# Cross attention: folding the queries of two heads over 64 rows each, into two banks

## The chip, the cores and the metric

The kernel runs on one core of a Trainium2 chip. The metric is the time of one execution on the device in microseconds (us), as the median over several runs. The engines of a core are named as in the profile: PE multiplies matrices (PEld are its weight loads), DVE does vector work, ACT activations and copies, POOL general work and gathers, SP issues transfers. PE writes its results into eight PSUM banks, each 128 partitions by 512 float32 numbers.

## What is computed

The reference is a stack of six parts on a residual stream `x` of 16 batches x 64 rows x 256 numbers: a sampled cross attention, a self attention and an expert layer, then a second cross attention, a recurrent layer and a second expert layer. The change lies in the second cross attention, with 16 heads of 64:

```python
q = (x @ Wq).reshape(B, N, HEADS, DIM_HEAD)
k = (ctx_txt @ Wk).reshape(B, TEXT_LEN, HEADS, DIM_HEAD)
v = (ctx_txt @ Wv).reshape(B, TEXT_LEN, HEADS, DIM_HEAD)
out = _attend(q, k, v)
Li = ctx_img.shape[1]
k_ip = (ctx_img @ Wk_ip).reshape(B, Li, HEADS, DIM_HEAD)
v_ip = (ctx_img @ Wv_ip).reshape(B, Li, HEADS, DIM_HEAD)
out_ip = _attend(q, k_ip, v_ip)
out = out + IMG_SCALE * out_ip
return out @ Wo + bo
```

`ctx_txt` are the first 77 rows of a batch's context, `ctx_img` the other 1524. `_attend` is a softmax attention with the scale 1/8.

## The kernel before, in words

For the 1524 image rows the kernel does not form the keys. It folds the key weights of a head into that head's queries instead: q k^T = (q Wk_ip^T) ctx^T, so the folded queries, 256 numbers for each of 64 queries, are multiplied with the turned context directly. The values are treated in the same way: the probabilities are multiplied with the context itself, and the value weights come after.

The class `Cross` does this in steps. A step is one pair of heads of one batch: 16 batches x 8 pairs = 128 steps, in the order of the counter `n`. In a step the 128 columns are 2 heads x 64 queries. Engines PE, DVE and ACT run in the order in which the code is written; nothing reorders it. A step `n` (line 1124 on) issues, for PE:

- 24 matmuls that give the scores of pair `n` (line 88, `st<-qf,cT`): 12 chunks of 128 context rows, two halves of 256, into three banks of their own pool of four. After each bank DVE takes a maximum (line 1144). Between the second and the third bank stands the turning of the result of pair `n - 2`.
- `out(n - 2)` (line 1074): value weights for two heads, each into 64 partitions of one bank.
- the product of probabilities and context of pair `n - 1`, in three parts of four chunks each (line 1113), into one bank that stays open over all three parts. Between the first and second part stands the transpose of the maximum (line 1163), and between the second and third part its transpose back (line 1173) and `fold(n + 2)`.

After line 1173 ACT copies the maximum (`mc`, line 1175), then `fold`'s result (line 1072); DVE subtracts `mc` from the scores (line 1184) and ACT takes the exponential (line 1185) of each of three banks in turn. These are the probabilities `pt` that the next step's product reads. `step` takes up to four generators of other stages' work (`side`, `mid`, `more`, `late`), which put their own instructions in between; the one called `late` stands between the exponentials and the third part of the product.

The fold of a pair works on `qbd`, a tile that holds for each pair and batch a block diagonal: partitions 0 to 63 have the first head's 64 queries in columns 0 to 63 and zeros in the others, partitions 64 to 127 the second head's in columns 64 to 127. The zeros are written once, when the tiles are made; `queries` (line 1009) fills only the blocks. With the zeros, one matmul over all 128 partitions (64 rows of the key weights of one head and 64 of the other) gives both heads' folded queries side by side, 128 columns. There are two such matmuls a fold, one for each half of the 256 context numbers, and their result is copied in one piece. The same tile `qbd`, zeros and all, is what `text` (line 1031) takes as its stationary side for the 77 text rows.

The weights come as `wk`, four pairs in one tile, loaded from memory by SP two times a batch. Two folds are issued ahead of the first step, in `ahead` (line 1221). All matmul results but the scores share a pool of four banks, taken with `bank()`; a bank is free again once what reads it is done.

Of the kernel before, what the change touches and what calls it, by code (L numbers as in the profile page):

```python
# [17 lines left out]
P = 128  # L18
B, S, D = 16, 64, 256
M = 1601  # L20
KC = D // P
# [13 lines left out]
H1, HD1, INNER, TEXT = 16, 64, 1024, 77  # L35
# [30 lines left out]
def perceiver_kernel(ctx: ExitStack, tc: tile.TileContext, a: dict, out: bass.AP):  # L66
    nc = tc.nc

    def mk(pool, shape, tag, dtype=F32, bufs=None):
        return pool.tile(list(shape), dtype, tag=tag, name=tag, bufs=bufs)  # L70
# [71 lines left out]
    def bank():  # L142
        return mk(pmm, [P, 512], "mm")
# [73 lines left out]
    qbds = []  # L217
# [51 lines left out]
    for j in range(2):  # L269
        r = slice(j * S, (j + 1) * S)  # L270
# [688 lines left out]
    class Cross:  # L959
# [100 lines left out]
        def fold(self, n):  # L1060

            if n >= B * NHP:
                return
            b, hp = divmod(n, NHP)
            w = self.w[b, hp // 4]
            rhs = qbds[b // 2 % 2][:, hp, b % 2].rearrange("p h q -> p (h q)")
            pf = bank()
            for k in range(KC):
                nc.tensor.matmul(pf[:, k * P : (k + 1) * P], lhsT=w[:, hp % 4, k * P : (k + 1) * P], rhs=rhs,  # L1069
                                 start=True, stop=True)  # L1070
            qf = self.qf[n] = mk(self.xc, [P, KC, P], "qf", bufs=3)
            nc.scalar.copy(qf.rearrange("p c n -> p (c n)"), pf[:, : KC * P])  # L1072

        def out(self, n):

# [788 lines left out]
```

## Time and profile before

| what | value |
|---|---|
| time, median of 3 runs | 2980.36 us (2976.62 to 2980.77) |
| profiled execution | 2978.07 us, of which 2976.4 us are its span |
| PE busy | 2811.3 us, 94% of the span |
| PEld busy | 2344.9 us, 79% |
| DVE busy | 1626.4 us, 55% |
| ACT busy | 1071.7 us, 36% |
| POOL busy | 830.4 us, 28% |
| share of the chain of waits that lies on PE | 76% |
| granted clock of PE, mean | 0.98 |
| fold's matmuls, line 1069 | records of 275 ns in the median, 762.6 to 2655.0 us, and 8 records before that |
| fold's copy, line 1072 | 128 copies of 128x256, 373 ns each |

A profile of this kind lists, for one execution, every instruction with its engine, its line in the kernel, the tiles it writes and reads, and its duration. Sizes such as `128*128 128x257` at a matmul mean 128 rows and 128 columns of the stationary side, and a moving side of 128 rows by 257 columns. Every float32 matmul has two records, each with a weight load. Matmuls overlap, and their ends are modelled: a record's duration is longer than the time by which it puts off the next, so distances between starts say more than durations. The chain of waits follows the execution back from its last instruction; what stands in it sets the end. The windows table gives each engine's busy time in stretches of the execution, and the timeline merges equal instructions that follow each other into one row with their number.

### The profile page before, as it was taken

Reading aid. Unit: us, or ns where it says so; the run is one execution under the profiler, and the core shown is the slowest. Engines: PE = TensorE matmul, PEld = TensorE weight load, DVE = VectorE, ACT = ScalarE, POOL = GpSimd, SP = SyncE. Lnnn points to the kernel's source line nnn. Section 1 sums busy time; section 2 is a strip of 40 time slices with the busy share of each in tenths; the row PEclk is TensorE's granted clock in tenths of the full one; section 3 lists DMA queues with packets and bytes.
Section 4 is the critical chain, followed back from the end, with each engine's and each line's share of the span. In section 5 each row is a group of like instructions: output and inputs, shape, how many; then the busy total and the mean of one; then the engine's idle time right before and its main releaser. Section 6 shows DMA issues by size and latency. Waiting matters only on the chain.

```text
span 2976.4 us, 46295 instructions
## 1 busy us (share of the span) xinstructions
PE 2811.3 (94%) x17734; PEld 2344.9 (79%) x17734; DVE 1626.4 (55%) x4138; ACT 1071.7 (36%) x2427; POOL 830.4 (28%) x923
## 2 busy tenths in 40 slices
PE   8999999796899988999999999999999999997799
PEld 4554466464788877899999999999999999994687
DVE  3344443533566655332557754686544785655856
ACT  3443433542223443333343332443232443222431
POOL 0677777777771000000101100020000010001723
PEclk9999999998899999999999999999999999999999
DMA  7666766476322101465212111121111221005753
GB/s 218 180 193 201 225 184 195 137 236 183 77 69 63 49 10 41 135 192 167 70 50 80 52 33 52 55 71 55 38 33 47 66 64 51 8 1 161 218 151 110
DMA packets 324853, 313.97 MB, mean 105 GB/s; under 512 B 57989, under 2 KB 275881, under 8 KB 324121
## 3 DMA queue, kind: packets, MB, share of 16 engines
q1 hardware_dynamic: 172137, 213.05, 22.5%
q10 hardware_dynamic: 126928, 63.06, 7.5%
q0 software_dynamic: 25568, 34.91, 5.3%
q8 instruction: 141, 2.31, 0.3%
q14 instruction: 79, 0.65, 0.1%
HBM read 236.31 MB, written 74.62 MB: 104 GB/s over the span
## 4 chain that ended last, share of the span: by engine, by line
PE 76%; DVE 8%; POOL 6%; issue 3%; DMA 3%; ACT 3%; SPq 1%; ACTq 0%; DVEq 0%; POOLq 0%
PE st L88 31%; PE mm L1113 21%; PE mm L88 14%; POOL g L446 6%; PE mm L153 4%; PE mm L1069 2%; DMA g<-tab,ig 2%; DVE hs L1359 1%; PE mm L1099 1%; DVE hc L1364 1%; PE mm L1038 1%; ACT pt L1185 1%; DVE db L1357 1%; DVE mp L1144 1%; PE mm L1163 1%
## 5 line engine op out<-in xcount | busy, mean ns | idle before, releaser
L1113 PE MATMUL mm<-cn,pt 128*128 128x257 f32 (+1 forms) x3072 | 741.6, 385 | 1.2 <-ACT cT L82 1.2
L88 PE MATMUL st<-qf,cT 128*128 128x128 f32 x6144 | 739.9, 278 | 0.0
L88 PEld LDWEIGHTS st<-qf,cT 128*128 128x128 f32 x6144 | 721.3, 194 | 3.3 <-ACT qf L1072 0.2
L446 POOL DMA_INDIRECT g<-tab,ig x640 | 620.2, 969 | 282.1 <-issue 176.9
L1113 PEld LDWEIGHTS mm<-cn,pt 128*128 128x128 f32 (+1 forms) x3072 | 555.4, 190 | 84.6 <-ACT cT L82 2.3
L88 PE MATMUL st<-wkv,cxt 128*128 128x512 f32 (+1 forms) x832 | 377.1, 598 | 1.0 <-ACT cxt L415 1.0
L1144 DVE TENSOR_REDUCE mp<-st 128x128 f32<-128x512 f32 x384 | 260.4, 688 | 214.5 <-PE st L88 214.1
L1184 DVE TENSOR_TENSOR pt<-st,mc 128x512 f32<-128x512 f32 (+1 forms) x384 | 224.2, 639 | 152.2 <-ACT mc L1175 152.2
L88 PEld LDWEIGHTS st<-wkv,cxt 128*128 128x128 f32 (+1 forms) x832 | 149.1, 187 | 157.6 <-issue 155.9
L1185 ACT ACTIVATE pt<-pt 128x512 f32<-128x512 f32 (+1 forms) x384 | 207.5, 588 | 51.9 <-DVE pt L1184 51.6
L399 ACT COPY kv<-st 128x512 f32<-128x512 f32 (+1 forms) x208 | 121.3, 588 | 190.2 <-PE st L88 189.6
L1175 ACT COPY mc<-mm 128x128 f32<-128x128 f32 x128 | 34.2, 267 | 385.3 <-PE mm L1173 384.8
L972 POOL MEMSET cn<- 128x12 f32 x16 | 2.0, 122 | 590.6 <-PE mm L1113 584.1
L1122 ACT COPY ot<-mm 128x256 f32<-128x256 f32 x128 | 47.5, 371 | 311.2 <-PE mm L153 311.1
L1165 DVE TENSOR_REDUCE xmx<-mm 128x1 f32<-128x128 f32 x128 | 37.4, 292 | 193.4 <-PE mm L1163 193.4
L1465 POOL DMA_INDIRECT xb<-xnd,row x55 | 59.6, 1084 | 281.8 <-PE mm L1099 217.8
L1365 POOL TENSOR_TENSOR mn<-mn,hc 128x512 f32<-128x512 f32 x64 | 84.1, 1314 | 173.4 <-DVE hc L1364 165.2
L1089 ACT COPY yt<-mm 128x64 f32<-128x64 f32 x128 | 27.2, 213 | 248.4 <-PE mm L88 248.4
L88 PEld LDWEIGHTS mm<-xt,w 128*128 128x128 f32 x512 | 83.0, 197 | 26.0 <-issue 14.4
L88 PE MATMUL mm<-xt,w 128*128 128x256 f32 (+1 forms) x512 | 94.8, 333 | 3.3 <-DVE act L886 3.3
L1347 POOL MEMSET da<- 128x8 f32 x64 | 7.5, 117 | 319.3 <-ACT da L1346 319.0
L1359 DVE TENSOR_TENSOR_SCAN hs<-da,db 128x512 f32<-128x512 f32 x64 | 79.3, 1239 | 7.0 <-DVE db L1357 0.5
(469 smaller groups left out, 3978.1 us busy)
## 6 DMA issues: line engine op xcount, KB each, us to landing
tab<-kv ACTq DMA_DIRECT2D x48, 1024.0 KB
w<-in_gate SPq DMA_DIRECT2D x66, 512.0 KB
cx<-in_ctx SPq DMA_DIRECT2D x48, 512.0 KB
cn<-in_ctx SPq DMA_DIRECT2D x16, 1408.0 KB
w<-in_lin SPq DMA_DIRECT2D x33, 512.0 KB
wk<-in_xwkiT SPq DMA_DIRECT2D x32, 512.0 KB
wg<-in_guT SPq DMA_DIRECT2D x55, 256.0 KB
g<-tab,ig POOLq DMA_INDIRECT x640
```

What stands on the lines that cost most here:

```text
L88: nc.tensor.matmul(o, lhsT=l, rhs=r, start=i == 0, stop=i == len(pairs) - 1)
L153: nc.tensor.transpose(t[:ncol, i, :rows], b, ident[:rows, :rows])
L399: nc.scalar.copy(kv[:w, :, c, :], pk[:w].rearrange("p (h e) -> p h e", h=H0))
L446: nc.gpsimd.indirect_dma_start(out=gf[:, (half * n + s) * 4 * HD0 : (half * n + s + 1) * 4 * HD0], out_offset=None, in_=tables[j], in_offs ...
L1069: nc.tensor.matmul(pf[:, k * P : (k + 1) * P], lhsT=w[:, hp % 4, k * P : (k + 1) * P], rhs=rhs, start=True, stop=True)
L1113: nc.tensor.matmul(po, lhsT=pt[:w, c, :], rhs=cn[:w, c, :], start=c == 0, stop=c == NCH - 1)
L1144: nc.vector.tensor_reduce(mp_[:, i, :], s.rearrange("p c n -> p n c"), AX.X, ALU.max)
L1184: nc.vector.tensor_tensor(o, st[i][:, :m, :], mc.to_broadcast([P, m, P]), ALU.subtract)
L1185: nc.scalar.activation(o, o, AF.Exp)
L1359: nc.vector.tensor_tensor_scan(hs.rearrange("p c n -> p (c n)"), da.rearrange("p c n -> p (c n)"), db.rearrange("p c n -> p (c n)"), 0.0, ...
L1365: nc.gpsimd.tensor_tensor(y, y, hc, ALU.add)
L1465: nc.gpsimd.indirect_dma_start(out=x, out_offset=None, in_=xnd, in_offset=bass.IndirectOffsetOnAxis(ap=tb.row[:, i : i + 1], axis=0))
```

## The change

The fold no longer multiplies over all 128 partitions with the zeros in. Each head gets matmuls of its own, over its own 64 partitions of the weights and of `qbd`, with 64 moving columns in place of 128. The two heads take turns, and each writes into a bank of its own, so a fold takes two of the four banks. Its result is copied in two pieces, one for each head, into the same tile `qf` as before.

```diff
-            rhs = qbds[b // 2 % 2][:, hp, b % 2].rearrange("p h q -> p (h q)")
-            pf = bank()
+            pf = [bank(), bank()]
+
             for k in range(KC):
-                nc.tensor.matmul(pf[:, k * P : (k + 1) * P], lhsT=w[:, hp % 4, k * P : (k + 1) * P], rhs=rhs,
-                                 start=True, stop=True)
+                for h in range(2):
+                    r = slice(h * HD1, (h + 1) * HD1)
+                    nc.tensor.matmul(pf[h][:, k * S : (k + 1) * S], lhsT=w[r, hp % 4, k * P : (k + 1) * P],
+                                     rhs=qbds[b // 2 % 2][r, hp, b % 2, h, :], start=True, stop=True)
             qf = self.qf[n] = mk(self.xc, [P, KC, P], "qf", bufs=3)
-            nc.scalar.copy(qf.rearrange("p c n -> p (c n)"), pf[:, : KC * P])
+            for h in range(2):
+                nc.scalar.copy(qf[:, :, h * S : (h + 1) * S], pf[h][:, : KC * S].rearrange("p (k q) -> p k q", q=S))
```

Here `KC` is 2, `P` 128, `S` 64 (queries of a batch) and `HD1` 64 (size of a head). The tile `qbd`, its zeros and `text`, which reads them, are left as they were.

## The prediction

> **What bounds the kernel now.** I read the busy table first, then the windows table over the stretch in which the changed function runs, then the chain of waits, and last the timeline of one step. The changed function, `fold`, has the line 1069 (its matmuls) and 1072 (its copy); it runs from 753 to 2655 us.
>
> ```profile
> core 0: us, PE busy (x) PEld busy (x) DVE busy (x) ACT busy (x) POOL busy (x), PEclk, DMA share, GB/s
> 762.00:955.00 193.00, 183.18 (x1371) 168.43 (x1369) 129.78 (x332) 57.30 (x143) 108.89 (x118) 0.98 0.24 61
> 955.00:1160.00 205.00, 182.20 (x1202) 163.35 (x1203) 118.25 (x372) 91.39 (x196) 0.12 (x1) 0.93 0.11 34
> 1160.00:2676.00 1516.00, 1507.06 (x11252) 1387.84 (x11251) 880.50 (x2020) 523.33 (x1247) 94.76 (x144) 1.00 0.22 66
> ```
>
> The reader is to see that from 1160 us on PE is idle for 9 of 1516 us, at a granted clock of 1.00; DVE and ACT have 42% and 65% to spare. The chain of waits in one step of this stretch is PE alone:
>
> ```profile
> 1508.23 0.11 PE mm L1173
> 1508.34 0.45 PE mm L1069 x4
> 1508.78 1.74 PE mm L1113 x8
> ```
>
> So what is added to PE's stream between line 1173 and line 1113 is added to the end, step by step. Now PE and its weight loads (PEld) around that fold:
>
> ```profile
> 1508.07 0.27 PE L1173 MATMUL mm<-ident,xmx 128*128 128x128 f32 x1
> 1508.07 0.52 PEld L1069 LDWEIGHTS mm<-qbd,wk 128*128 128x128 f32 x4
> 1508.17 0.61 PE L1069 MATMUL mm<-qbd,wk 128*128 128x128 f32 x4
> ...
> 1508.51 0.96 PEld L1113 LDWEIGHTS mm<-cn,pt 128*128 128x128 f32 x5
> 1508.62 1.03 PE L1113 MATMUL mm<-cn,pt 128*128 128x257 f32 x4
> ```
>
> Each f32 matmul leaves two records, each with a load of its own: two matmuls, x4. One load lasts 0.192 us, so four loads in 0.52 start (0.52 - 0.19) / 3 = 0.11 us apart. The first load starts together with the matmul before it (1508.07 both), and line 1113's first load together with fold's last matmul (1508.17 + 0.61 - 0.275 = 1508.505). Loads are hidden behind the matmuls ahead of them. From the transpose of line 1173 to the product's first matmul it is 1508.62 - 1508.07 = 0.55 us; in nearly all of the 126 steps that fold it is the same within 0.01.
>
> **What the narrower moving side is worth.** After the change each matmul moves 64 columns in place of 128, but its stationary side keeps 128 columns. What such a record costs is seen where the moving side is narrow already, in a router product with 8 columns:
>
> ```profile
> 568.17 0.52 PEld L88 LDWEIGHTS mm<-rws,xt 128*128 128x128 f32 x4 [1.28 <-ACT xt L173]
> 568.18 0.61 PE L88 MATMUL mm<-rws,xt 128*128 128x8 f32 x4 [1.05 <-ACT xt L173]
> ```
>
> Four loads in 0.52 again: 0.11 us apart, with 8 moving columns as with 128. The load sets the pace. So halving the moving side saves nothing by itself, and the change makes 8 records of 4. Run one after another they take 8 x 0.11 = 0.89 us in place of 0.44.
>
> **Two halves side by side.** The eight are two independent sets of four: rows 0 to 63 for one head, rows 64 to 127 for the other, each into its own bank. Before has no matmul on a row half, but it has one on column halves in the same order (two records on the first, two on the second):
>
> ```profile
> 18.11 0.19 PEld L291 LDWEIGHTS mm<-dg,ones 16*64 16x64 f32 x4 [0.76 <-issue]
> ```
>
> A load of 64 columns lasts 0.13 and back to back they start 0.055 apart (two of line 88's in 0.19), so one after another four would take 0.13 + 3 x 0.055 = 0.30. They took 0.19: two and two at a time. I take the row halves as running side by side too: 4 x 0.11 = 0.44 us, what fold takes now. The bound above is 0.89, the bound below 4 x 0.055 = 0.22, if half the rows loaded in half the time, as half the columns do.
>
> **The change of shape.** The step already leaves the full array once, for `out`, whose results go to 64 partitions:
>
> ```profile
> 1502.10 0.50 PE L88 MATMUL st<-qf,cT 128*128 128x128 f32 x3
> ...
> 1502.81 0.45 PE L88 MATMUL mm<-ot,wvi 128*64 128x64 f32 x6
> ...
> 1502.53 0.19 PEld L88 LDWEIGHTS mm<-ptt,vt 77*64 77x64 f32 x2
> ...
> 1502.70 0.19 PEld L88 LDWEIGHTS mm<-ptt,vt 77*64 77x64 f32 x2
> ...
> 1503.19 0.51 PEld L1113 LDWEIGHTS mm<-cn,pt 128*128 128x128 f32 x3
> ```
>
> Going in: the last full matmul starts at 1502.10 + 0.50 - 0.275 = 1502.325, and the next load not with it but at 1502.53, 0.205 later. Coming out: the last half-wide matmul starts at 1502.81 + 0.45 - 0.22 = 1503.04, the next load at 1503.19, 0.15 later. Neither load is hidden: the array first runs empty. Over all steps of the trace these two gaps hold within 0.01 us, also where the load waits for no semaphore, so it is the shape and not a wait.
>
> Fold gets both. After: 0.205 until the first load, 0.11 for that load, 3 x 0.11 to the last matmul's start, 0.15 until the product's load, 0.11 for it: 0.905 us. Less 0.555: +0.35 us a fold. Between the two heads' tiles the shape stays, so I count nothing there (the column halves above show none).
>
> The Trainium skill bears on this at one place. No row of before has a row half; its page "TensorEngine Tiling (Array Packing)", section "Key Properties", says that a change of tiling mode drains the engine and a change of tile within a mode doesn't. By it the sum stands, +0.35. The same page's table of theoretical speedups gives up to twice the rate where the contraction is 64 or less; by that alone fold would go from 0.44 to an estimated 0.22 us. The load rows here, 0.11 us with 8 moving columns, are why I don't take it.
>
> **The sum.** 128 folds (as many copies of line 1072): 126 inside steps, two ahead of the first, which share one change of shape. 126 x 0.35 + 0.4 = 44.5 us. Eleven of them lie between 955 and 1160 us, where PE has 23 us of idle time, much of it for side chains of other engines; I let a third of their delay vanish there: -1.3. Sum +43 us.
>
> **What is hidden.** One copy of 256 columns (line 1072, 373 ns) becomes two of 128. The nearest row is line 1175, 267 ns: 2 x 267 - 373 = +161 ns a fold on ACT, 20 us in all. Behind them on ACT stand the exponentials of line 1185, which wait for DVE's first subtraction (from 1508.67, 0.69 us) anyway; PE needs their result at the next step's product, over 5 us later, and qf two steps later. Cover: ACT's idle 65%. Without that cover it would be +20 us. The second bank: of the four that matmuls share, the product's and the maximum's are taken at fold, so the two heads take the others, which ACT's copy in `out` and DVE's reduction have left microseconds earlier. Who comes next into these banks waits for ACT's second copy, some 0.75 us after fold; PE has 1.74 us of product to run first. In some 17 steps side work stands in between, its first bank is the maximum's, free by then; bound 17 x 0.75 = 13 us, taken as 0. The zeros are still written once, and `text` still reads them: nothing is saved there. No DMA moves.
>
> The profiled execution had 2976.4 us of span, 2978.07 in all, 2.3 under the median of 2980.36. On the median: **2980.4 + 43 = 3023 us**. Offsets between the halves of 0.11 (one record) or 0.17 (what `out`'s second half shows, 1502.70 against 1502.53) give +0.46 or +0.52 a fold, 3038 or 3046.
>
> **Rivals.**
> - The halves do not overlap: 8 x 0.11. Then +0.35 + 0.445 = +0.79 us a fold, +100 us, 3080. Against it: the column halves above. For it: a load of 128 columns sets the pace, and two may share one path; no row shows two of that width at once.
> - No draining for row halves: 0.44 against 0.44, no change, 2980. Against it: every smaller shape in the trace shows such gaps, those of 16, 17 and 23 rows (lines 291 and 653) among them: 0.10 to 0.13 us from their last matmul to the next load.
> - The other side: half the rows load in half the time, and the array isn't drained. 0.22 us less a fold, 128 x 0.22 = 28 us less: 2952. It decides from a fold of under 0.50 us between line 1173 and the product, 6 us in all. For it: the 64-column loads at half the pace; against it: both its parts must hold.
> - ACT as the bound: +20 us on top, 3043; against it its idle share.
>
> **Chances.** Side by side with draining, 3016 to 3030: 0.66. With an offset or with ACT's copies in the open, to 3046: 0.13. One after another: 0.10. No change: 0.04. Faster: 0.05. The rest, between 2990 and 3012: 0.02. About 0.2% (6 us) is what a measurement here can tell from no change. Range 3012 to 3046 holds the first two, 0.79. Slower: 0.66 + 0.13 + 0.10 + 0.02 = 0.91.
>
> **What would show it.** In the timeline, fold's first load starts 0.20 us after line 1173's transpose and not with it; its matmuls come in pairs a few ns apart, pairs 0.11 apart; the product's first load comes 0.15 after the last. Line 1113's share of the chain stays, PE's busy time grows by some 43 us or less (modelled ends hide the empty array), two copies of about 267 ns stand per fold. Wrong if the pairs are 0.055 apart, if eight starts are evenly 0.11 apart, or if the loads start with the matmul before them.

## The result: slower by 39 us, and the profile after

The changed kernel takes 3018.25 us (median of 4 runs, 3011.67 to 3020.12); before took 2979.03 us (median of 4, 2976.62 to 2980.77). The ratio is 1.0128, with a 95% interval of 1.011 to 1.0146. The profiled execution has a span of 3018.4 us, 42.0 more than that of before.

The windows table of the changed kernel, over the late part of the stretch with folds (columns: the window, its length, busy time and instructions of each engine, granted clock, share and rate of transfers):

```profile
core 0: us, PE busy (x) PEld busy (x) DVE busy (x) ACT busy (x) POOL busy (x), PEclk, DMA share, GB/s
1160.00:2718.00 1558.00, 1549.63 (x11682) 1402.67 (x11682) 889.11 (x2037) 530.14 (x1350) 94.73 (x144) 1.00 0.21 65
```

PE is still idle for only 8 us, at a granted clock of 1.00; DVE's busy time rises by 9 and ACT's by 7 us. The stretch is 42 us longer, and PE fills it. At its start the changed kernel is already 7 us behind (the 25th transpose of its line 1176 starts at 1165.0 us, before's 25th of line 1173 at 1158.5). From the first of these transposes to the last it takes 43.6 us more than before; the first one starts 2.2 us earlier. The timeline of one step of the changed kernel, around the fold (its line is now 1071, the transpose's 1176, the product's 1116):

```profile
1801.62 0.27 PE L1176 MATMUL mm<-ident,xmx 128*128 128x128 f32 x1
...
1801.82 0.52 PEld L1071 LDWEIGHTS mm<-qbd,wk 64*128 64x128 f32 x8 [0.28 <-issue]
1801.82 0.66 PE L1071 MATMUL mm<-qbd,wk 64*128 64x64 f32 x8
1801.98 0.27 ACT L1178 COPY mc<-mm 128x128 f32<-128x128 f32 x1 [3.74 <-PE mm L1176]
...
1802.41 0.95 PEld L1116 LDWEIGHTS mm<-cn,pt 128*128 128x128 f32 x5
1802.41 1.14 PE L1116 MATMUL mm<-cn,pt 128*128 128x257 f32 x4
1802.51 0.43 ACT L1075 COPY qf<-mm 128x128 f32<-128x128 f32 x2 [0.26 <-PE mm L1071]
```

Three things are to be seen. Eight loads take 0.52 us, as four did before: they run two and two, (0.52 - 0.19) / 3 = 0.11 us from pair to pair; in the single records the two loads of a pair start 6 to 7 ns apart. The first load starts 0.20 us after the transpose, where before it started with it. And the product's first load comes 1802.41 - 1801.62 = 0.79 us after the transpose, where before it came 0.44 after; now it isn't hidden either, for the product's first matmul record starts with it. In the single records, which the timeline merges, the product's second matmul starts 1.11 us after the transpose, 0.77 before: +0.34 us a fold, and 126 x 0.34 = 43 us. The chain of waits has the same place:

```profile
1801.78 0.11 PE mm L1176
1801.89 0.59 PE mm L1071 x8
1802.48 1.94 PE mm L1116 x8
```

Before it stood there as 0.11, 0.45 and 1.74: the fold's piece is 0.14 longer and the product's, which now holds a load that nothing hides, 0.20.

### The profile page after: what moved, and what is told of

Same layout as the page of the kernel before. It is cut to its first block, busy times and chain, and to the rows that moved or that the text cites. A ratio compares the mean times of both kernels' runs of the same rounds, so it can differ in the third digit from the quotient of the medians.

```text
span 3018.4 us, 47507 instructions
## 1 busy us (share of the span) xinstructions
PE 2857.2 (95%) x18246; PEld 2355.1 (78%) x18246; DVE 1633.7 (54%) x4138; ACT 1080.3 (36%) x2555; POOL 827.5 (27%) x923
## 4 chain that ended last, share of the span: by engine, by line
PE 82%; DVE 6%; POOL 3%; DMA 3%; ACT 3%; issue 2%; SPq 1%; ACTq 0%; DVEq 0%; POOLq 0%
PE st L88 34%; PE mm L1116 23%; PE mm L88 15%; PE mm L153 5%; POOL g L446 3%; PE mm L1071 3%; DMA g<-tab,ig 1%; PE mm L1102 1%; PE mm L1038 1%; DVE hs L1362 1%; DVE hc L1367 1%; PE mm L1166 1%; ACT pt L1188 1%; PE mm L1176 0%; DVE db L1360 0%
## 5 line engine op out<-in xcount | busy, mean ns | idle before, releaser
L1116 PE MATMUL mm<-cn,pt 128*128 128x257 f32 (+1 forms) x3072 | 756.2, 390 | 1.0 <-ACT cT L82 1.0
L1071 PEld LDWEIGHTS mm<-qbd,wk 64*128 64x128 f32 x1008 | 68.1, 187 | 36.1 <-issue 31.0
```

The source lines that it names most:

```text
L1071: nc.tensor.matmul(pf[h][:, k * S : (k + 1) * S], lhsT=w[r, hp % 4, k * P : (k + 1) * P], rhs=qbds[b // 2 % 2][r, hp, b % 2, h, :], start= ...
L1116: nc.tensor.matmul(po, lhsT=pt[:w, c, :], rhs=cn[:w, c, :], start=c == 0, stop=c == NCH - 1)
```

## The experiments

All experiments ran on three other chips than the first comparison. On these the same kernel before took 3265 to 3299 us: the part up to the first fold is some 225 to 255 us longer there and scatters. So each whole time is compared with before on its own chip, and beside it I give a stretch in which PE is hardly ever idle (busy for 1195.7 of 1200.1 us in before): the 87 steps from the 41st transpose of line 1173 to the last (starts of records in the trace; for before 1478.79 and 2678.86 us). Before took 1200.1 us for it on the first chip and again 1200.1 on a later one, after 1228.1 on both. It holds 86 folds; in e6 the fold's new place leaves 85.

| kernel | whole, us | before on the same chip, us | ratio (95% interval) | 87 steps, us | against before |
|---|---|---|---|---|---|
| after, first chip | 3018.25 | 2979.03 | 1.0128 (1.011 to 1.0146) | 1228.1 | +28.0 |
| a0_after_again | 3309.58 | 3266.67 | 1.0139 (1.0105 to 1.0173) | 1228.1 | +28.0 |
| e1_full_rows | 3358.04 | 3299.13 | 1.0176 (1.0138 to 1.0213) | 1236.7 | +36.6 |
| e2_one_half | 3381.7 | 3299.13 | 1.0241 (1.0211 to 1.0272) | 1264.1 | +64.0 |
| e3_two_a_visit | 3325.81 | 3299.13 | 1.0069 (1.0032 to 1.0106) | 1214.9 | +14.8 |
| e4_two_copies | 3297.84 | 3299.13 | 1.0005 (0.9977 to 1.0034) | 1200.1 | 0.0 |
| e5_head_by_head | 3312.9 | 3265.41 | 1.0148 (1.0107 to 1.0189) | 1228.6 | +28.5 |
| e6_after_out | 3305.04 | 3265.41 | 1.011 (1.0071 to 1.0148) | 1210.7 | +10.6 |
| e7_two_batches | 3281.79 | 3265.41 | 1.0047 (1.0023 to 1.007) | 1197.1 | -3.0 |
| e8_two_batches_after_out | 3277.27 | 3265.41 | 1.0029 (1.0007 to 1.0052) | 1188.5 | -11.6 |
| e9_two_batches_full | 3278.09 | 3266.67 | 1.0039 (1.0008 to 1.007) | 1197.9 | -2.2 |
| e10_late_start | 3267.95 | 3266.67 | 1.001 (0.9992 to 1.0028) | 1188.5 | -11.6 |

In e7 to e10 the 87 steps hold less work: 40 visits, which are 80 folds and not 86, since six pairs of heads of the stretch were folded ahead of it. At 0.44 us a fold of before that alone is 6 x 0.44 = 2.7 us. For these kernels a second stretch counts: from the turning of a result (`mm<-ident,os`) in step 46 to that in step 126, 80 steps with 80 folds in every kernel.

| kernel | 80 steps with equal work, us | against before |
|---|---|---|
| before (both chips) | 1104.9 | |
| after (both chips) | 1130.9 | +26.0 |
| e6_after_out | 1115.3 | +10.4 |
| e7_two_batches | 1104.6 | -0.3 |
| e8_two_batches_after_out, e10_late_start | 1096.1 | -8.8 |
| e9_two_batches_full | 1105.4 | +0.5 |

**The load's pace alone.** Four narrow matmuls a fold, but over all rows, so that the shape never changes:

```diff
-                    r = slice(h * HD1, (h + 1) * HD1)
-                    nc.tensor.matmul(pf[h][:, k * S : (k + 1) * S], lhsT=w[r, hp % 4, k * P : (k + 1) * P],
-                                     rhs=qbds[b // 2 % 2][r, hp, b % 2, h, :], start=True, stop=True)
+                    nc.tensor.matmul(pf[h][:, k * S : (k + 1) * S], lhsT=w[:, hp % 4, k * P : (k + 1) * P],
+                                     rhs=qbds[b // 2 % 2][:, hp, b % 2, h, :], start=True, stop=True)
```

> Four matmuls a fold with 64 moving columns each, into two banks, but over all 128 rows, zeros included: no change of shape. Theory (a load of 128 columns sets a pace of 0.11 us, a smaller shape empties the array): eight loads one after another, 0.89 us in place of 0.44, no empty array: +0.445 x 126 = +56 on before, 3035. Rival (half the moving columns take half the time): as before, 2979.

Timeline of this kernel (its fold is line 1070, the transpose 1175, the product 1115):

```profile
2366.54 0.27 PE L1175 MATMUL mm<-ident,xmx 128*128 128x128 f32 x1
2367.49 1.52 PE L1115 MATMUL mm<-cn,pt 128*128 128x257 f32 x6
...
2366.54 0.97 PEld L1070 LDWEIGHTS mm<-qbd,wk 128*128 128x128 f32 x8
```

Eight loads in 0.97: (0.97 - 0.19) / 7 = 0.11 apart, though each matmul moves half as many columns. The first starts with the transpose: no gap. From the transpose to the product's matmul it is 0.95, +0.40 on before; 36.6 / 86 = 0.43 a fold in the 87 steps, and +59 in the whole where 56 were expected. The rival falls: narrower moving sides are worth nothing under a load of 128 columns. Twice the records without the two halves are dearer than the change.

**The overlap taken away.** Both heads' matmuls on rows 0 to 63 (with another pair's weights for the second, so that no load repeats); the second head's queries are left out:

```diff
+            r = slice(0, HD1)
             for k in range(KC):
                 for h in range(2):
-                    r = slice(h * HD1, (h + 1) * HD1)
-                    nc.tensor.matmul(pf[h][:, k * S : (k + 1) * S], lhsT=w[r, hp % 4, k * P : (k + 1) * P],
-                                     rhs=qbds[b // 2 % 2][r, hp, b % 2, h, :], start=True, stop=True)
+                    nc.tensor.matmul(pf[h][:, k * S : (k + 1) * S], lhsT=w[r, (hp + h) % 4, k * P : (k + 1) * P],
+                                     rhs=qbds[b // 2 % 2][r, hp, b % 2, 0, :], start=True, stop=True)
```

> All four matmuls of a fold on rows 0 to 63, so the second head's queries are not folded: nothing can run side by side. Theory: the empty array of after stays (0.34 us a fold), and eight loads follow one another, 0.44 us more: 126 x 0.785 = +99 on before, 3078. Rival (64 rows load in half the time, and nothing runs side by side in after either): as after, 3018.

Timeline of this kernel:

```profile
2369.99 0.27 PE L1176 MATMUL mm<-ident,xmx 128*128 128x128 f32 x1
...
2370.19 0.96 PEld L1071 LDWEIGHTS mm<-qbd,wk 64*128 64x128 f32 x8 [0.28 <-issue]
2371.22 0.95 PEld L1116 LDWEIGHTS mm<-cn,pt 128*128 128x128 f32 x5
```

The same two gaps (0.20 going in), and between them eight loads one after another: 0.96 where the change has 0.52. The 87 steps grow by 64.0 / 86 = 0.74 us a fold, 0.79 expected; the whole by 83, less than the 99 expected, with an interval that leaves 70 to 90. Rows of 64 load no faster than rows of 128: the rival falls. What after gains by running side by side is thus 1264.1 - 1228.1 = 36 us in these steps.

**The emptying halved.** Two folds together in every second step; `pf` is viewed as two folds by two halves of the context numbers:

```diff
-            self.fold(n + 2)
+            if n % 2:
+                self.fold([n + 1, n + 2])
```

> As after, but two folds together in every second step, into the same two banks. Theory: the array is emptied half as often, 63 x 0.34 = +21 on before, 3000. Rival (the loss lies in the number of records or copies): unchanged, 3018.

Timeline of this kernel (fold 1072, transpose 1178, product 1118):

```profile
2369.36 0.27 PE L1178 MATMUL mm<-ident,xmx 128*128 128x128 f32 x1
2369.56 1.11 PE L1072 MATMUL mm<-qbd,wk 64*128 64x64 f32 x16
...
2370.60 0.95 PEld L1118 LDWEIGHTS mm<-cn,pt 128*128 128x128 f32 x5
```

Sixteen records, twice those of the change, and the product's load comes 1.24 us after the transpose: 0.45 more than the change's 0.79 and not twice it. The 87 steps lose 14.8 instead of 28.0, close to the half. The cost goes by visits, not by records, matmuls or copies. The whole lost 27, with an interval from 11 to 35; 21 were expected.

**The copies alone.** Before's two matmuls and one bank, with the copy in two pieces:

```diff
-            nc.scalar.copy(qf.rearrange("p c n -> p (c n)"), pf[:, : KC * P])
+            for h in range(2):
+                nc.scalar.copy(qf[:, :, h * S : (h + 1) * S],
+                               pf[:, : KC * P].rearrange("p (k h q) -> p k h q", k=KC, h=2)[:, :, h, :])
```

> Before, with ACT's copy alone made in two pieces. Theory: hidden, 2979, within 3. Rival (ACT's longer queue holds up the exponentials): up to +20, 2999.

1.0005, and the 87 steps agree with before to the tenth. ACT's 20 us are hidden; nothing of the loss is theirs.

**The order of the heads.** The two loops changed round:

```diff
-            for k in range(KC):
-                for h in range(2):
+            for h in range(2):
+                for k in range(KC):
```

> As after, but both matmuls of the first head stand ahead of both of the second: four records on one half, then four on the other. Theory: PE looks ahead past a busy half, as in the step's out; the second half starts at most 0.17 us late: 3018 to 3040. Rival (records start in the order of the program): the halves follow one another, +0.44 x 126 on after for the most part, 3055 to 3074.

Timeline of this kernel:

```profile
2332.30 0.67 PE L1071 MATMUL mm<-qbd,wk 64*128 64x64 f32 x8
...
2332.30 0.53 PEld L1071 LDWEIGHTS mm<-qbd,wk 64*128 64x128 f32 x8 [0.28 <-issue]
```

Eight loads in 0.53 again, though four for the first half stand ahead of four for the second; on one half alone eight took 0.96 (e2). "In turns" isn't needed: records of the second half start beside those of the first, not behind them. So the order of the code does not fix the order of the starts. The names in before's `out` show the same: the second head's loads `ptt` start at 1502.70 us, though six more records of `ot` follow, two of them the first head's. 1228.6 against 1228.1 in the 87 steps.

**The fold moved behind `out`**, which has left the full array already:

```diff
                 self.out(n - 2)
+            self.fold(n + 2)
...
-            self.fold(n + 2)
```

> As after, but the fold stands right behind out, whose matmuls already left the full array: the array is emptied three times a step in place of four. Theory: from out's last matmul the fold adds its own loads and one emptying, 0.59 us, in place of 0.44 in before: +0.15 x 126 = +19 on before, 2998. Rival (going from column halves to row halves costs as much as through the full array): 3018.

Timeline of this kernel, from `out` to the product:

```profile
2006.49 0.45 PE L88 MATMUL mm<-ot,wvi 128*64 128x64 f32 x6
...
2006.87 0.52 PEld L1071 LDWEIGHTS mm<-qbd,wk 64*128 64x128 f32 x8
2007.46 1.17 PEld L1116 LDWEIGHTS mm<-cn,pt 128*128 128x128 f32 x6
```

From column halves to row halves the gap is there too (last matmul 2006.49 + 0.45 - 0.22 = 2006.72, next load 2006.87: 0.15), so it is paid at this change of shape too. But the way back from `out` was paid before, so the fold adds only 2007.46 - 2006.87 = 0.59. In the 87 steps it loses 10.6 us, 0.12 a fold, 0.15 expected; after lost 28.0. The whole lost 40 and not 19, as much as the rival would: its first 12 steps (from the first transpose to the 13th) took 227 us. With the fold at its old place in every step they took 199 to 215 (b0, a0, e5, e4, e1, e2), but also 223 in e3, where it stands in every second. That is what the last runs looked into.

**Two batches in a visit.** Batches 2t and 2t + 1 use the same weights and lie side by side in `qbd`. Folding both at once gives 128 moving columns, so that the load's pace is no longer wasted:

```diff
+                    nc.tensor.matmul(pf[h][:, k * q : (k + 1) * q].rearrange("p (b q) -> p b q", q=S),
+                                     lhsT=w[r, hp % 4, k * P : (k + 1) * P],
+                                     rhs=qbds[b // 2 % 2][r, hp, bs[0] : bs[-1] + 1, h, :], start=True, stop=True)
...
+                if bb:
+                    qf = mk(self.xp, [P, KC, P], "qo", bufs=8)
```

> Row halves with 128 moving columns: the two batches of a pair share the weights, so one visit in the even batch's steps folds both, and the odd batch's steps fold nothing; 62 visits instead of 126. The folded queries of the odd batch wait in 8 tiles, paid for with single buffers for the weights and the text values. Theory: a visit costs 0.79 us where two folds of before cost 0.89: -0.1 x 62 = -6 on before, 2973. Rival (two halves cannot move 128 columns each side by side): +0.44 a visit, 3001.

> As the run with two batches in a visit, but the visit stands right behind out. Theory: 0.59 us a visit where two folds of before cost 0.89: -0.3 x 62 = -18 on before, 2960, faster than both kernels. Rival (no gain from the shared emptying): 2973.

> Two batches in a visit as in e7, with the same buffers and loads, but over all 128 rows with the zeros, 256 moving columns: no change of shape. Control for what the grouping alone does. Theory: four records at the pace of 256 columns, 0.217 us, 0.87 us a visit where two folds of before cost 0.89: the 87 steps from the 41st transpose of line 1173 to the last as in before, 1200 us, within 2, and the whole as before. Rival (e7 and e8 gain by the halved weight loads or the fewer visits and not by the row halves): as e7, 1197, or less.

Timelines of e7 and of e9, both with the visit at the old place:

```profile
2316.35 0.27 PE L1191 MATMUL mm<-ident,xmx 128*128 128x128 f32 x1
2316.55 0.71 PE L1079 MATMUL mm<-qbd,wk 64*128 64x128 f32 x8
...
2317.19 1.39 PEld L1131 LDWEIGHTS mm<-cn,pt 128*128 128x128 f32 x7
```

```profile
2331.09 0.27 PE L1188 MATMUL mm<-ident,xmx 128*128 128x128 f32 x1
2331.20 1.03 PE L1077 MATMUL mm<-qbd,wk 128*128 128x256 f32 x4
...
2331.85 1.49 PEld L1128 LDWEIGHTS mm<-cn,pt 128*128 128x128 f32 x7
```

The row halves move 128 columns each side by side: two folds in place of the change's one, 0.05 us later at the product's load (0.84 after the transpose, 0.79 in the change). The rival of e7 falls. At the old place neither form gains: on equal work e7 is 0.3 us below before and e9, the same grouping with the zeros, 0.5 above, so the emptying takes what the row halves save. The 3.0 and 2.2 us of the 87 steps are little more than the six folds made ahead; by these steps alone e9 stands between its theory (1200, within 2) and its rival (1197), on equal work it stands with its theory.

Behind `out`, in e8:

```profile
2072.19 0.45 PE L88 MATMUL mm<-ot,wvi 128*64 128x64 f32 x6
2072.57 0.71 PE L1079 MATMUL mm<-qbd,wk 64*128 64x128 f32 x8
2073.22 1.14 PE L1131 MATMUL mm<-cn,pt 128*128 128x257 f32 x4
```

A visit takes 2073.22 - 2072.57 = 0.65 us, not the 0.59 of e6's 64 columns, against 0.89 for two folds of before. On equal work e8 saves 8.8 us, 0.22 for each of 40 visits, 0.30 expected. So in the stretch that PE bounds, e8 is faster than both kernels. The whole times missed their expectations: e7, e8 and e9 are 0.3 to 0.5% slower than before on their chips.

**Where e8 gave it back.** e10 is e8 with the visit at its old place in the first 12 steps:

```diff
+            if n >= 12:
+                self.fold(n + 2)
...
+            if n < 12:
+                self.fold(n + 2)
```

> Two batches in a visit right behind out, as e8, but in the first 12 steps, where gathers and loads run beside, the visit keeps its old place. Theory: the 87 steps as e8, 1188.5 us, 11.6 below before; the first 12 steps no longer than before's; the whole 15 to 18 below before on the same chip. Rival (the loss of e8's first steps is not the place of the fold): the first 12 steps some 10 us longer than before's again, the whole within 5 of before.

> The changed kernel, unaltered, on the same chip as the two above. Theory: the 87 steps take 1228 us, 28 more than before, whatever the chip; the whole +39 to +43 on before. Rival (on a chip with slower transfers the early stage takes part of it up): less than +30 in the whole.

> Before, unaltered, for its profile on the same chip: the first 12 steps and the 87 late steps to set beside the others. Both theories: 87 steps in 1200 us; the time up to the first fold as in the three above, within 15.

Before again (b0) and after again (a0) repeat the 87 steps to the tenth, and after's +43 on before in the whole is what the first chip showed. From the 13th transpose to the end e10's profile takes 2047.5 us, b0's 2064.7: 17 less, what was expected of the whole. Its first 12 steps took 208 us, e8's 225, b0's 199, a0's 208; e7 and e9, with the visit at the old place throughout, 207 and 209. But the medians of the whole are equal, 1.001 with an interval of 0.9992 to 1.0028. So what e10's rival named came true: first steps 9 us longer than b0's, and a whole within 5 us of before. The profiled run of e10 is 10 us under its median, b0's 4 over its own; where the other runs lose what the late steps gain, most likely up to the 13th step, is not shown. Gathers and weight loads run in that stage, whole runs of one kernel scatter by 20 us and more, and there is one profile of each: it stays open. No version was shown to be faster than before as a whole. None of e6 to e10 was tried on a chip on which the early stage is as short as in the first comparison.

## Why the prediction was right

- **PE is the bound.** Right: the added time stands in PE's stream between the transpose and the product, and from the first transpose to the last the kernel grew by what was added there (43.6 us; 126 x 0.34 = 43). The spacing of 0.55 us was read as nearly the same in all 126 steps; it holds in 106, and in 19 others side work stands between.
- **The narrower moving side saves nothing.** Right, and shown by itself: e1's eight loads are 0.11 us apart at 64 columns as before's four at 128.
- **The halves run side by side.** Right: two and two, 6 to 7 ns apart. It was taken from one row with column halves. e2 shows what it is worth, and the rival of 3080 us as it would have looked. Offsets of 0.11 or 0.17 us between the halves did not come, in either order of the heads (6 to 7 ns; in e5 12 to 14).
- **The array empties at each change of shape.** Right for row halves as for column halves, and e3 and e6 show it by itself. This is what the Trainium skill, "TensorEngine Tiling (Array Packing)", section "Key Properties", says of a change of tiling mode; these runs agree, with 0.15 to 0.20 us at each change. Of the up to twofold rate that its table gives for a contraction of 64, these runs show both sides: against the same eight records on one half (e2, 0.96 us of loads) the halves side by side take 0.52, but that is what before's four records with the zeros took. Only with 128 moving columns (e7) did two folds run at that pace.
- **The sum.** The split was off and the sum not: the last matmul starts 0.39 us after the first load and not 0.44, and the way out takes 0.20 and not 0.15. Together 0.59, as worked out: that the two misses of 0.05 cancel is luck. The 1.3 us that were to vanish between 955 and 1160 us did not show: the 12 steps from the 13th transpose to the 25th grew by 4.8 us, 0.40 each, though in single profiles of a stage that scatters. A fold came to +0.34 (0.35 expected), the whole to +42.0 in the profiled pair and +39 in the medians (+43).
- **Copies and banks hidden.** Right: e4 for the copies. For the banks, the only wait of the changed profile on ACT's copy of line 1075 is one of 2.1 us at a transpose; the bound was 13.
- **The faster rival** needed loads of half the rows in half the time. e2 rules that out: 0.11 us each.

## What to carry to other kernels

Before splitting a matmul to skip zeros, look at what paces it: here the stationary load did, and skipping half the moving columns freed nothing. A tiled shape has a fixed price at each way in and out of it, 0.34 us a visit here. Doing two folds in a visit only won that back (e7); behind a stage that had already left the full array it saved 0.22 us a visit in the late steps (e8), and no whole run was shown to be faster.

## What the runs showed of the hardware that was not expected

Two row halves keep the full array's pace with 128 moving columns each (e7: eight loads in 0.52 us, as four over all rows in before). In that time they make two folds, where the full array made one, since half of what it multiplied was zeros. PE pairs them up in both orders tried (e5). And a stretch that PE bounds repeats to 0.1 us in 1200 from one chip to another, while the stage before it, with transfers and gathers, took some 225 to 255 us more on the three other chips.
